# Cross-attention with image-prompt keys on one Trainium2 core: the last query chunk and the last key chunk of an odd batch moved ahead of the next batch's projections

## The chip, the cores and the metric

The kernel runs on one core of one Trainium2 chip. A core has a matrix engine (TensorE, in the profile PE, with its weight loads listed apart as PEld), a vector engine (VectorE, DVE), a scalar engine (ScalarE, ACT), GpSimd (POOL) and a queue engine that issues transfers (SyncE, SP). The metric is the device time of one execution in microseconds. Before the change the median of three runs is 409.02 us (408.52 to 409.29).

## The reference, cut to what matters

Eight batches (B = 8), 112 queries each (S), 375 context rows of 512 channels (T, E): 371 text rows and 4 image-prompt rows. C = 320 channels in H = 20 heads of 16.

```python
q = heads(hidden_states @ W_q);  k_t = heads(text_ehs @ W_k);  v_t = heads(text_ehs @ W_v)
probs_t = softmax(q @ k_t.T * Dh ** -0.5)
text_out = probs_t @ v_t
k_ip = heads(ip_ehs @ W_k_ip);  v_ip = heads(ip_ehs @ W_v_ip)
attn_scores = q @ k_ip.T * Dh ** -0.5
qsem = l2norm(probs_t @ text_ehs)              # per head, 512 channels
sem = qsem @ l2norm(ip_ehs).T
probs_ip = softmax(attn_scores + 0.5 * sem) * spatial_mask
out = (text_out + probs_ip @ v_ip) @ W_out + b_out + hidden_states
```

The norm of `qsem` is never formed from its 512 channels. With G = text_ehs @ text_ehs.T it is the sum of p * (G p), so the kernel multiplies the transposed probabilities by a matrix that holds G, the prompt products and the head's values side by side.

## The kernel before, in words

All data are float32. The work is a run of 40 steps (b, g): batch b, group g of four heads, five groups a batch. One step does the following.

* `scores` (line 789): four matmuls, one for each head of the group, into four PSUM banks. They read `kT`, the batch's transposed keys in three chunks of channels, and `qm`, its masked queries, in the same three chunks. Groups 0 to 3 read chunks 0 and 1. Group 4 alone reads the last chunk.
* `probabilities`: DVE takes the row maximum (802), ACT the exponential (806) and a small copy of the prompt columns (808), and SP writes the result into the buffer `xg` (813). After the copy the PSUM bank is free.
* `transposed` (825): DVE turns `xg` into `xgT`.
* `product` (837): 12 blocks j of four matmuls each, `xgT` by `u`, into four PSUM banks `ps_qd`. `u` is filled by transfers (547) and by POOL copies of the values (`placed`, 755).
* `value_sums` (ACT, 864) and `reduced` (DVE, 890) read the four banks and so free them.

The order of every engine's instructions is written out by hand; nothing is scheduled by a planner. After the first step the loop takes two steps at a time. `pair` issues the products of the two steps, and during the first two blocks of the first one the scores of the step that comes two later. Between pairs `behind` issues all other matrix work: projections of queries, keys and values, the Gram matrix G, and the pieces of `finish`, a generator (called as `f`) that ends a batch step by step. `q`, `k` and `v` are such generators too, one chunk a call. In the branch that the change touches, `k(nb)` is a chunk of the next batch's keys with a copy on ACT (563, 570), `v(nb)` the seven block products of the next batch's values (`two_chunks`, 663) with seven copies on ACT (664) and seven sums on POOL (667), `q(b)` the last chunk of this batch's queries, scaled on DVE (376, 386), and `k(b)` the last chunk of this batch's keys, copied by ACT in four parts (580, 590). `tr(0)` transposes all of the coming step, `tr(1)` half of the one after it.

That branch runs behind group 1 of every odd batch except the last: for b = 1, 3 and 5. The pair that follows starts with step (b, 2), and the scores in it are those of (b, 4), the group that reads the last chunks.

There are eight PSUM banks in three pools: four `qd`, two `sc`, two `mm`. The list `turn` names the pool from which each call of `bank` in `behind` takes its bank, in order. A bank can be written again when its last reader is done.

ACT switches between two tables, for square roots and for exponentials, with explicit loads (`preload_act_table`, lines 1427 and 1432 in this branch).

Of the kernel before, what the change touches and what calls it, by code (L numbers as in the profile page):

```python
# [9 lines left out]
AF = mybir.ActivationFunctionType  # L10
# [10 lines left out]
def kernel(  # L21
# [14 lines left out]
    nc = tc.nc  # L36
# [52 lines left out]
    turn = []  # L89
# [258 lines left out]
    def turned_inputs(bs, i0=0, i1=NC):  # L348

        t0, n = blocks_of(bs)  # L350
        if bs[0] not in inputs_turned:
            inputs_turned[bs[0]] = work.tile(
                [P, NC, 2 * S], F32, tag="xT", name=f"xT_{bs[0]}", bufs=1
            )
        xT = inputs_turned[bs[0]]
        nc.vector.transpose(
            xT[:, i0:i1, : n * RG].rearrange("p i (j r) -> p j i r", r=RG),
            x_in[:, :n, i0 * RG : i1 * RG].rearrange("p j (i c) -> p j i c", c=RG),
        )
# [53 lines left out]
    def load_next(b):  # L413
        if 2 <= b < B:
            loaded[b] = load_ctx(b)
# [127 lines left out]
    def gram_to_groups(b, blocks, eng=nc.sync):  # L543

        for q in blocks:
            for a in range(GROUP):
                eng.dma_start(
                    st[b]["u"][a * RG : (a + 1) * RG, q * GW : (q + 1) * GW],
                    ug[q * RG : (q + 1) * RG, :],
                )  # L550
# [5 lines left out]
    def keys(b):  # L556
        s = st[b]
        if b > 1:
            prompt_keys(b)
        for i in range(FULL):  # L560
            ps = bank(f"ps_k_{b}_{i}")
            for e in range(NE):
                nc.tensor.matmul(  # L563
                    ps[:, :TT],
                    wk_sb[:, e, i * P : (i + 1) * P],
                    s["ctxT"][:, e, :TT],
                    start=(e == 0),
                    stop=(e == NE - 1),
                )
            nc.scalar.copy(s["kT"][:, i, :TT], ps[:, :TT])  # L570
            yield
        last_keys(b, bank(f"ps_k_{b}_{FULL}", spare=0 < b < B - 1))
        yield
# [21 lines left out]
    def values(b):  # L595
        s = st[b]
        s["vext"] = work.tile([P, NT, C], F32, tag="vext", name=f"vext_{b}", bufs=1)
        ctxT, vext = s["ctxT"], s["vext"]
        if b > 1 and b % 2 == 0:
            two_chunks(b)  # L600
            yield
        for c in range(0 if b < 2 else 2, NT):
            ps = bank(f"ps_v_{b}_{c}")
            for e in range(NE):
                nc.tensor.matmul(  # L605
                    ps[:, :C],
                    ctxT[:, e, c * P : (c + 1) * P],
                    wv_sb[:, e, :],
                    start=(e == 0),
                    stop=(e == NE - 1),  # L610
                )
            nc.scalar.copy(vext[:, c, :], ps[:, :C])
            yield
        if b > 1 and b % 2:
            two_chunks(b)
            yield
# [98 lines left out]
    def prompt_values(b):  # L715

        nc.sync.dma_start(
            st[b]["vip"].rearrange("p n h d -> p (n h d)"),
            vipd[b * NIP : (b + 1) * NIP, :].rearrange("n c -> (n c)").partition_broadcast(S),
        )  # L720
# [94 lines left out]
    def transposed(b, g, j0=0, j1=BLK):  # L815

        xg = x_ring[(b * NG + g) % NX]
        if j1 < j0 + 1:
            return
        if ("xT", g) not in st[b]:  # L820
            st[b]["xT", g] = work.tile([P, BLK, P], F32, tag="xgT", name=f"xgT_{b}_{g}")
        xT = st[b]["xT", g]
        n = BLK // (2 if b == B - 1 or (b, g) == (0, 0) or j1 - j0 < BLK else 1)
        for j in range(j0, j1, n):
            nc.vector.transpose(  # L825
                xT[:, j : j + n].rearrange("p j (k q) -> p q j k", q=QN),
                xg[:, :, j * RG : (j + n) * RG].rearrange("p q (j k) -> p q j k", k=RG),
            )
# [317 lines left out]
    def run(key, make, pieces=1):  # L1146

        if key not in gens:
            gens[key] = make()
        for _ in range(pieces):  # L1150
            next(gens[key], None)
# [56 lines left out]
    def f(b, pieces=1):  # L1208
        if b >= 0:
            run(("f", b), lambda: finish(b), pieces)  # L1210

    def k(b, pieces=1):
        run(("k", b), lambda: keys(b), pieces)

    def v(b, pieces=1):
        run(("v", b), lambda: values(b), pieces)

    def gr(b, pieces=1):
        run(("g", b), lambda: gram(b), pieces)
# [116 lines left out]
    def behind(n):  # L1336

        b, g = steps[n]
        nb = b + 1
        two = steps[n + 1 : min(n + 3, len(steps) - NG + 1)]  # L1340

        def tr(i):
            if i < len(two):
                transposed(*two[i], 0, BLK // (1 + i))

        if b % 2 == 0 and g == 0:
            if n == 0:
                turn[:] = ["sc", "sc", "mm"]
                turned_inputs(pairs[1])
            else:  # L1350
                turn[:] = ["qd"] * 4 + ["mm"]
                k(b)
                nc.scalar.preload_act_table(AF.Sqrt)
                f(b - 1)
                if b - 1 < B - 2:
                    prompt_values(b - 1)
            if n:
                token_sums(nb)
                gr(nb)
                tr(0)  # L1360
            if n:
                gr(nb, 2)
                f(b - 1)
            v(nb)
            if n == 0:
                k(nb)
                run(("pp",), prompt_projections)
            if n:
                tr(1)
                f(b - 1, 2)  # L1370
            load_next(b + 2)
        elif b % 2 == 0 and g == 2:
            turn[:] = ["qd"] * (8 if b else 3) + ["mm"]
            gram_to_groups(nb, (2,))
            if b == 0:
                run(("pp",), None)
                prompt_keys(nb)
                tr(0)
                v(nb)
                q(nb)  # L1380
                values_to_dram(nb, nc.scalar, 0, 2)
                v(nb)
                values_to_dram(nb, nc.scalar, 2)
                run(("pp",), None)
            else:
                values_to_dram(nb, nc.gpsimd, 2)
                k(nb)
                tr(0)
                v(nb)
                q(nb)  # L1390
                values_to_dram(nb, nc.gpsimd, 0, 2)
            tr(1)
        elif b % 2 == 0 and nb < B - 1:
            turn[:] = ["qd"] * (4 + (b > 0)) + ["mm", "mm"]
            turned(b + 2)
            token_sums(b + 2)
            q(nb)
            if b > 0:
                f(b - 1)
            else:  # L1400
                run(("t", b), lambda: prompt_logits(b))
            k(nb)
            tr(0)
            if b > 0:
                f(b - 1)
            gr(nb + 1, 3)
            if b > 0:
                f(b - 1)
            if n + 1 not in late:
                tr(1)  # L1410
            load_next(b + 3)
            f(b)
            prompt_values(b)
        elif b % 2 == 0:
            turn[:] = ["qd"] * 4 + ["mm"]
            q(nb, 2)
            f(b - 1)
            k(nb)
            nc.scalar.preload_act_table(AF.Sqrt)
            tr(0)  # L1420
            f(b - 1, 2)
            prompt_values(b)
            f(b, 2)
        elif g == 1:
            turn[:] = ["qd"] * 8 + ["sc", "mm"]
            gram_to_groups(nb, (2,))
            nc.scalar.preload_act_table(AF.Sqrt)
            f(b - 1)
            k(nb)
            tr(0)  # L1430
            v(nb)
            nc.scalar.preload_act_table(AF.Exp)
            q(b)
            k(b)
            f(b - 1)
            tr(1)
            f(b - 1)
            values_to_dram(nb, nc.sync, 0, 2)
            if b == B - 3:
                prompt_values_by_head()  # L1440
        else:
            turn[:] = ["qd"] * 3 + ["sc"]
            load_turned(nc.gpsimd, pairs[(b + 3) // 2])
            v(nb)
            f(b - 1)
            values_to_dram(nb, nc.sync, 2)
            tr(0)
            k(nb)
            f(b - 1, 2)
            tr(1)  # L1450
            gram_to_groups(nb, (3,))
            values_to_groups(nb, 2)
        assert not turn, (b, g, turn)

    for n in range(0, len(steps) - NG, 2):
# [4 lines left out]
        b, g = steps[n]  # L1460
# [16 lines left out]
    b = B - 1  # L1477
# [125 lines left out]
```

## Time and profile before

| | |
|---|---|
| median of three runs | 409.02 us |
| the profiled execution | 407.42 us |
| its span, first to last instruction | 405.7 us |
| PE busy | 398.3 us (98% of the span) |
| DVE busy | 329.1 us (81%) |
| ACT busy | 198.8 us (49%) |
| POOL busy | 182.8 us (45%) |
| granted TensorE clock | 0.999 |
| the branch's stretch, from its first key matmul to the next pair's first product | 95.24 to 103.71, 191.67 to 200.15, 287.46 to 295.93 us |

Times inside the profile are microseconds from the first instruction. A busy PE is one that has a matmul in flight, which is less than one at its peak. A row of a timeline reads: start, duration, engine, line, operation, output and inputs, shape, count, and in brackets the idle time before it with what ended it. In the chain of waits, the work that ended last is followed back from the end; a row is start, duration and what it was.

### The profile page before, as it was taken

What the parts mean: (1) busy time and instruction counts of PE and PEld (TensorE: products, weight loads), DVE (VectorE), ACT (ScalarE), POOL (GpSimd) and SP (SyncE); (2) the same over time, 40 slices, a digit from 0 to 9 for tenths busy, and PEclk for the clock granted to TensorE, in tenths of its full rate; (3) what the DMA queues carried; (4) which work ended last, traced back from release to release, by engine and by line L of the source; (5) the groups of instructions that cost most, each with busy time, mean ns of one, the idle gap of its engine ahead of it and who ended that gap; (6) DMA issues with size and microseconds to landing.
All of it is one profiled execution on the core that took longest, in us unless ns stands there. A gap on an engine that the chain in (4) does not pass through costs nothing.

```text
span 405.7 us, 14386 instructions
## 1 busy us (share of the span) xinstructions
PE 398.3 (98%) x5673; PEld 322.0 (79%) x5673; DVE 329.1 (81%) x703; ACT 198.8 (49%) x707; POOL 182.8 (45%) x391
## 2 busy tenths in 40 slices
PE   8999999999999999999999999999999999999996
PEld 7868688888777887978786878878877878887894
DVE  4457689866998897987899898897789898888984
ACT  3245332336542843525653564334654385446764
POOL 8735012063281558141554338523337155804681
PEclk9999999999999999999999999999999999999999
DMA  8969756969665966577647766667856444776311
GB/s 244 228 179 251 138 154 169 206 137 215 159 173 153 215 148 178 135 180 165 179 122 171 182 170 167 161 164 163 190 141 169 121 124 110 190 176 175 110 53 28
DMA packets 58390, 65.85 MB, mean 162 GB/s; under 512 B 20165, under 2 KB 51641, under 8 KB 58324
## 3 DMA queue, kind: packets, MB, share of 16 engines
q1 hardware_dynamic: 54814, 58.23, 57.7%
q0 software_dynamic: 2336, 5.42, 5.5%
q10 hardware_dynamic: 1174, 1.29, 1.0%
q8 instruction: 45, 0.74, 0.8%
q14 instruction: 21, 0.17, 0.2%
HBM read 20.22 MB, written 5.22 MB: 63 GB/s over the span
## 4 chain that ended last, share of the span: by engine, by line
PE 92%; DMA 4%; POOL 1%; ACT 1%; DVE 0%; issue 0%; POOLq 0%
PE ps_qd L837 44%; PE ps_k L563 10%; PE ps_s L789 7%; PE ps_g L533 7%; PE ps_v L605 7%; PE ps_vs L663 6%; PE ps_o L994 3%; PE ps_k L580 3%; PE ps_q L394 3%; DMA xg<-p 2%; DMA vr<-vd 1%; PE ps_g L495 1%; ACT kT L590 1%; DMA ct<-in_ctx_dram 1%; PE ps_c L464 1%; PE ps_a L985 1%
## 5 line engine op out<-in xcount | busy, mean ns | idle before, releaser
L837 PE MATMUL ps_qd<-u,xgT 32*112 32x232 f32 (+11 forms) x3840 | 217.8, 352 | 0.6 <-POOL u L755 0.5
L837 PEld LDWEIGHTS ps_qd<-u,xgT 32*112 32x112 f32 x3840 | 179.9, 172 | 31.7 <-issue 4.2
L825 DVE STREAM_TRANSPOSE xgT<-xg 128x768 f32<-128x768 f32 (+1 forms) x63 | 123.1, 1972 | 5.4 <-DMA xg<-p 4.7
L806 ACT ACTIVATE p<-ps_s,nmx 112x371 f32<-112x371 f32 x160 | 85.5, 585 | 63.0 <-DVE nmx L802 62.0
L802 DVE TENSOR_REDUCE nmx<-ps_s 112x1 f32<-112x371 f32 x160 | 76.8, 533 | 28.3 <-PE ps_s L789 26.7
L755 POOL COPY u<-vr 128x64 f32<-128x64 f32 x120 | 27.1, 238 | 159.8 <-PE ps_qd L837 90.0
L890 DVE CUSTOM_DVE_ANT_0 p<-ps_qd,p 112x371 f32<-112x371 f32 x152 | 73.5, 541 | 11.9 <-ACT pvs L864 7.4
L789 PE MATMUL ps_s<-kT,qm 32*112 32x375 f32 (+1 forms) x320 | 61.5, 487 | 1.6 <-ACT kT L590 1.6
L864 ACT COPY pvs<-ps_qd 112x21 f32<-112x21 f32 x152 | 21.8, 200 | 55.8 <-DVE ss L890 50.1
L563 PE MATMUL ps_k<-ctxT,wk_sb 128*128 128x371 f32 x128 | 43.4, 482 | 0.0
L789 PEld LDWEIGHTS ps_s<-kT,qm 32*112 32x112 f32 x320 | 27.4, 171 | 9.2 <-ACT kT L590 3.5
L563 PEld LDWEIGHTS ps_k<-ctxT,wk_sb 128*128 128x128 f32 x128 | 23.1, 190 | 12.2
L533 PE MATMUL ps_g<-ctxT 128*32 128x119 f32 (+11 forms) x672 | 32.7, 338 | 0.0
L533 PEld LDWEIGHTS ps_g<-ctxT 128*32 128x32 f32 x672 | 27.7, 109 | 6.1 <-POOL ctxT L440 0.9
L605 PE MATMUL ps_v<-wv_sb,ctxT 128*128 128x320 f32 x96 | 28.3, 441 | 0.0
L452 DVE STREAM_TRANSPOSE ctxT<-ct 128x512 f32<-128x512 f32 x21 | 22.5, 1084 | 4.1 <-DMA ct<-in_ctx_dram 4.1
L808 ACT COPY ipl<-ps_s 112x4 f32<-112x4 f32 x140 | 24.3, 173 | 0.0
L605 PEld LDWEIGHTS ps_v<-wv_sb,ctxT 128*128 128x128 f32 x96 | 17.5, 190 | 6.6
L570 ACT COPY kT<-ps_k 128x371 f32<-128x371 f32 x16 | 7.5, 466 | 23.1 <-PE ps_k L563 23.1
L973 POOL TENSOR_TENSOR vip<-vip,w 112x1280 f32<-112x1280 f32 (+1 forms) x8 | 17.5, 2182 | 0.2 <-DVE w L967 0.2
L517 POOL TENSOR_TENSOR ug<-ug,half 128x128 f32<-128x128 f32 (+1 forms) x24 | 10.6, 447 | 14.3 <-ACT ug L516 11.7
L512 ACT ACTIVATE ug<-ps_g 128x279 f32<-128x279 f32 (+5 forms) x24 | 8.0, 333 | 18.3 <-PE ps_g L533 13.4
(179 smaller groups left out, 439.4 us busy)
## 6 DMA issues: line engine op xcount, KB each, us to landing
xg<-p SPq DMA_DIRECT2D x159, 162.3 KB
u<-ug SPq DMA_DIRECT2D x120, 99.0 KB
ct<-in_ctx_dram SPq DMA_DIRECT2D x28, 176.0 KB
vip<-vipd SPq DMA_DIRECT2D x7, 560.0 KB
vr<-vd SPq DMA_DIRECT2D x20, 120.0 KB
out_dram<-ob SPq DMA_DIRECT2D x7, 140.0 KB
vr<-vd SPq DMA_DIRECT2D x12, 80.0 KB
x_in<-in_x_dram POOLq DMA_DIRECT2D x12, 70.0 KB, 3.7
```

The source lines that it names most:

```text
L533: nc.tensor.matmul(ps[p * RG : (p + 1) * RG, s0 : T - t0], ctxT[:, e, t0 + q * RG : t0 + (q + 1) * RG], ctxT[:, e, t0 + s0 : T], start=(e ...
L563: nc.tensor.matmul(ps[:, :TT], wk_sb[:, e, i * P : (i + 1) * P], s["ctxT"][:, e, :TT], start=(e == 0), stop=(e == NE - 1),)
L605: nc.tensor.matmul(ps[:, :C], ctxT[:, e, c * P : (c + 1) * P], wv_sb[:, e, :], start=(e == 0), stop=(e == NE - 1),)
L663: nc.tensor.matmul(ps[:, :CH], a[:, k], t[:, k], start=(k == 0), stop=(k == 1))
L755: nc.gpsimd.tensor_copy(region(b, c)[:, :, UV - c * P :], s["vr"][:, c * QN : (c + 1) * QN, g, :])
L789: nc.tensor.matmul(ps[:S, :w], qm[a * RG : (a + 1) * RG, i, r, j * S : (j + 1) * S], s["kT"][a * RG : (a + 1) * RG, i, :w], start=True, st ...
L802: nc.vector.tensor_reduce(nmx, ps[:S, :TT], AX.X, ALU.max, negate=True)
L806: nc.scalar.activation(p, ps[:S, :TT], AF.Exp, bias=nmx)
L808: nc.scalar.copy(s["ipl"][:, groups[g][a], :], ps[:S, TT:T])
L825: nc.vector.transpose(xT[:, j : j + n].rearrange("p j (k q) -> p q j k", q=QN), xg[:, :, j * RG : (j + n) * RG].rearrange("p q (j k) -> p ...
L837: nc.tensor.matmul(banks[a][:S, j * RG : UW], xT[a * RG : (a + 1) * RG, j, :S], region(b, c)[a * RG : (a + 1) * RG, p, q * RG :], start=(j ...
L890: nc.vector.tensor_tensor_reduce(out=p, in0=ps[:S, :TT], in1=p, scale=1.0, scalar=0.0, op0=ALU.mult, op1=ALU.add, accum_out=s["ss"][:, h : ...
```

## The change

Inside the branch for group 1 of an odd batch, the calls are put in another order. `q(b)` and `k(b)` come first, ahead of `k(nb)` and `v(nb)`. One call of `f(b - 1)` (the one that takes the square root and starts `zr`, `attn` and `xb`) now stands behind them and not at the start; the next call stands ahead of `v(nb)` and not behind `k(b)`. The load of the exponential's table comes right behind the square root. `turn` gives the ten banks so that the first seven are `qd` and the last three block products take `sc`, `mm` and `mm`; before, the first eight were `qd`, the queries took `sc` and the keys `mm`. No instruction is added or removed.

```diff
         elif g == 1:
-            turn[:] = ["qd"] * 8 + ["sc", "mm"]
+            turn[:] = ["qd"] * 7 + ["sc", "mm", "mm"]
             gram_to_groups(nb, (2,))
             nc.scalar.preload_act_table(AF.Sqrt)
-            f(b - 1)
-            k(nb)
-            tr(0)
-            v(nb)
-            nc.scalar.preload_act_table(AF.Exp)
             q(b)
             k(b)
             f(b - 1)
+            nc.scalar.preload_act_table(AF.Exp)
+            k(nb)
+            tr(0)
+            f(b - 1)
+            v(nb)
             tr(1)
             f(b - 1)
             values_to_dram(nb, nc.sync, 0, 2)
```

On PE, for b = 1, between the last product of step (1, 1) and the first scores of (1, 4). Before:

```order
L837 MATMUL ps_qd_1_1_1257<-u_274,xgT_1_1218 112x40
L563 MATMUL ps_k_0_1384<-ctxT_972,wk_sb 128x371 x4
L663 MATMUL ps_vs_1397<-wv_sb,ctxT_972 128x160 x2
...
L663 MATMUL ps_vs_1427<-wvt,ctxT_972 128x160 x2
L376 MATMUL ps_q_2_1433<-xT_589,wq_sb 64x112 x6
L580 MATMUL ps_k_2_1444<-ctxT_271,wk_sb 64x186
...
L837 MATMUL ps_qd_2_0_1472<-u_274,xgT_2_1390 112x392
...
L789 MATMUL ps_s_2_1480<-kT_272,qm_844 112x375
```

The same place now:

```order
L837 MATMUL ps_qd_1_1_1257<-u_274,xgT_1_1218 112x40
L376 MATMUL ps_q_2_1378<-xT_589,wq_sb 64x112 x6
L580 MATMUL ps_k_2_1389<-ctxT_271,wk_sb 64x186
...
L563 MATMUL ps_k_0_1409<-ctxT_972,wk_sb 128x371 x4
L663 MATMUL ps_vs_1429<-wv_sb,ctxT_972 128x160 x2
...
L663 MATMUL ps_vs_1459<-wvt,ctxT_972 128x160 x2
L837 MATMUL ps_qd_2_0_1472<-u_274,xgT_2_1415 112x392
...
L789 MATMUL ps_s_2_1480<-kT_272,qm_844 112x375
```

The six query matmuls and the eight matmuls of the last key chunk (one row of the eight is shown) moved from the end of the stretch to its start; the scores that read them stay where they were.

On ACT, from the load of the square root's table to the exponential of `finish`. Before:

```order
L1427 ACT_TABLE_LOAD
L939 ACTIVATE rn_1173<-rn_1173 112x20
L570 COPY kT_973<-ps_k_0_1384 128x371
L664 COPY v_2_1393<-ps_vs_1397 128x160
...
L664 COPY vext_1392<-ps_vs_1427 128x160
L1432 ACT_TABLE_LOAD
L590 COPY kT_272<-ps_k_2_1444 64x186 x2
L590 COPY kT_272<-ps_k_2_1444 64x185 x2
L959 ACTIVATE ex_1466<-fu_1458 112x80
```

Now:

```order
L1427 ACT_TABLE_LOAD
L590 COPY kT_272<-ps_k_2_1389 64x186 x2
L590 COPY kT_272<-ps_k_2_1389 64x185 x2
L939 ACTIVATE rn_1173<-rn_1173 112x20
L1431 ACT_TABLE_LOAD
L570 COPY kT_973<-ps_k_0_1409 128x371
L664 COPY v_2_1425<-ps_vs_1429 128x160
...
L664 COPY vext_1424<-ps_vs_1459 128x160
L959 ACTIVATE ex_1466<-fu_1418 112x80
```

The four copies into this batch's `kT` and the second table load moved ahead of the copy of the next batch's keys and of all seven copies of block products.

On DVE, in the same stretch, behind the four reductions of step (1, 1), as a difference:

```order
+L386 TENSOR_SCALAR qm_844<-ps_q_2_1378,emask 64x112 x4
 L942 RECIPROCAL zr_1175<-pvs_172 112x20
-L825 STREAM_TRANSPOSE xgT_2_1390<-xg_142 128x4x384
-L386 TENSOR_SCALAR qm_844<-ps_q_2_1433,emask 64x112 x4
+L825 STREAM_TRANSPOSE xgT_2_1415<-xg_142 128x4x384
 L949 RECIPROCAL rn_1173<-rn_1173 112x20
```

The four scalings into `qm` moved from behind the transposition of the coming step to a place ahead of it and of `zr`. POOL and SP keep their order.

## The prediction

> **What bounds the kernel now.** I read the page's busy times and chain first, then who waited for whom on PE, then the chain in order of time around the three places of the branch (b = 1, 3, 5; sites 1 to 3), then their timelines.
>
> ```profile
> PE 398.3 (98%) x5673; PEld 322.0 (79%) x5673; DVE 329.1 (81%) x703; ACT 198.8 (49%) x707; POOL 182.8 (45%) x391
> PE 92%; DMA 4%; POOL 1%; ACT 1%; DVE 0%; issue 0%; POOLq 0%
> PE ps_s L789 <- ACT kT L590: 1.6, 3, 0.5
> PEld ps_s L789 <- ACT kT L590: 3.5, 3, 1.2
> ```
>
> PE has almost no idle time and is 92% of the chain, so only what removes a stall of PE can help. The largest repeated one is three waits of scores for the copies of the last key chunk, one a site. PE counts 1.6 us idle, its weight loads 3.5 us; the true loss lies between, since matmuls are in flight for part of it. It can be read from the length of a whole pair. The chain in order of time:
>
> ```profile
> 102.53 1.28 PE ps_k L580 x16
> 105.16 0.57 PE ps_s L789 x2
> 115.90 2.35 PE ps_v L605 x8
> 141.65 1.15 PE ps_qd L837 x10
> 152.35 2.69 PE ps_k L563 x8
> 198.96 1.28 PE ps_k L580 x15
> 211.69 2.35 PE ps_v L605 x8
> 294.75 1.28 PE ps_k L580 x16
> 307.47 2.35 PE ps_v L605 x8
> ```
>
> A pair without this wait runs from 141.65 to 152.35, 10.70 us. The pairs behind the sites run from the end of their last key matmuls: 103.81 to 115.90 (12.09), 200.24 to 211.69 (11.45), 296.03 to 307.47 (11.44). All issue the same products and scores. So the excess is 1.39, 0.75 and 0.74 us, 2.88 in all. That is the most that the change can win here.
>
> **The change part by part.** Site 2 shows every part; its timeline:
>
> ```profile
> 191.67 2.76 PE L563 MATMUL ps_k<-ctxT,wk_sb 128*128 128x371 f32 x8
> 192.61 0.44 ACT L864 COPY pvs<-ps_qd 112x21 f32<-112x21 f32 x4
> 193.07 1.28 ACT L1427 ACT_TABLE_LOAD   x1
> 194.27 0.71 PE L663 MATMUL ps_vs<-wv_sb,ctxT 128*128 128x160 f32 x4
> 194.36 0.22 ACT L939 ACTIVATE rn<-rn 112x20 f32<-112x20 f32 x1
> 194.49 0.45 ACT L570 COPY kT<-ps_k 128x371 f32<-128x371 f32 x1
> 194.71 0.28 DVE L942 RECIPROCAL zr<-pvs 112x20 f32<-112x20 f32 x1
> 194.90 2.95 DVE L825 STREAM_TRANSPOSE xgT<-xg 128x1536 f32<-128x1536 f32 x1
> 196.44 0.71 PE L663 MATMUL ps_vs<-wv_sb,ctxT 128*128 128x160 f32 x4
> 198.17 0.80 PE L376 MATMUL ps_q<-xT,wq_sb 128*64 128x112 f32 x12
> 198.28 0.29 ACT L664 COPY vext<-ps_vs 128x160 f32<-128x160 f32 x1 [0.25 <-PE ps_vs L663]
> 198.79 1.42 PE L580 MATMUL ps_k<-ctxT,wk_sb 128*64 128x186 f32 x16
> 199.01 1.39 DVE L386 TENSOR_SCALAR qm<-ps_q,emask 64x112 f32<-64x112 f32 x4 [1.16 <-PE ps_q L376]
> 200.15 0.93 PE L837 MATMUL ps_qd<-u,xgT 32*112 32x392 f32 x8
> 200.27 1.27 ACT L590 COPY kT<-ps_k 64x186 f32<-64x186 f32 x4 [0.40 <-PE ps_k L580]
> 200.44 0.28 DVE L949 RECIPROCAL rn<-rn 112x20 f32<-112x20 f32 x1
> 201.59 0.57 PE L789 MATMUL ps_s<-kT,qm 32*112 32x375 f32 x2 [0.52 <-ACT kT L590]
> 201.75 1.57 DVE L825 STREAM_TRANSPOSE xgT<-xg 128x768 f32<-128x768 f32 x1
> ```
>
> *PE's stretch.* From start to start: next keys 2.60, seven block products 3.90, queries 0.62, last keys 1.36, together 8.48. In the new order queries start at 191.67, last keys at 192.29, next keys at 193.65, block products at 196.25, one each 0.54 ((196.44 - 194.27) / 4), and the first product again at 200.15. Changing the shape of the weights costs a little at each border; three borders are replaced by three others. I take 0; the largest idle time of the weight loads at such a border is quoted below (0.27 us), so the bound is 0.27 either way a site, 0.8 in all.
>
> *The wait itself.* ACT's copies of the last keys come behind the first table load: 194.35 to 195.62. The scales into `qm` follow DVE's last reduction, 194.71 to 196.10. The scores that need both come behind the product of 200.15. The wait of 0.75 is gone.
>
> *The new wait on ACT.* The copy of the next keys now stands behind four key copies (1.27), the square root (0.22) and the second load (1.28): 195.62, 195.84, 197.12, and with 0.45 it ends at 197.57. It frees a bank that a later block product takes: with four `qd` banks the fourth block product, due at 196.25 + 3 x 0.54 = 197.87. Margin 0.3 us. Queued behind this copy are the seven copies of block products. The first is due at about 197.0 and is 0.6 late, then they catch up at 0.29 each against PE's 0.54. Before, the seventh started on PE at 194.27 + 6 x 0.54 = 197.53 and its copy at 198.28; 1.98 later that copy ends at 200.55. Its `mm` bank is wanted by the scores of block 1, behind the 0.93 us of block 0, past 201. Cost 0; bounds 0 and what the slow rival below costs.
>
> *DVE.* `zr` and the transposition of the coming step slide back by 1.39: 196.3 to 199.3, and the product that needs it is at 200.15. At site 1 DVE idles before that transposition (first row of the next fence), which hides the scaling. What stood behind the scaling comes earlier: the five small operations of `finish` start at 199.3 and not 200.44, so the half transposition starts at 200.6 and not 201.75.
>
> *POOL and SP.* POOL's `attn` comes 1.39 us later, behind `zr`, and the sums of the block products at most the 1.98 us by which these move. SP's writes of the values wait for the sums, and behind them in its queue stand the rows of (b, 4). At site 3:
>
> ```profile
> 290.68 2.95 DVE L825 STREAM_TRANSPOSE xgT<-xg 128x1536 f32<-128x1536 f32 x1
> 296.29 2.22 SPq L699 DMA_DIRECT2D vd<-vext  x4
> 300.30 2.69 SPq L813 DMA_DIRECT2D xg<-p  x3
> ```
>
> At worst the writes start at 298.3 and end at 300.5, and the rows follow about a microsecond later than now. PE wants them in the pair that begins after 307.47. Cost 0.
>
> *Site 1's second excess.*
>
> ```profile
> 100.50 3.06 DVE L825 STREAM_TRANSPOSE xgT<-xg 128x1536 f32<-128x1536 f32 x1 [1.95 <-DMA xg<-p]
> 103.71 0.29 PEld L837 LDWEIGHTS ps_qd<-u,xgT 32*112 32x112 f32 x8 [0.27 <-POOL vext L667]
> 106.07 1.56 DVE L825 STREAM_TRANSPOSE xgT<-xg 128x768 f32<-128x768 f32 x1
> 107.67 1.89 DVE L802 TENSOR_REDUCE nmx<-ps_s 112x1 f32<-112x371 f32 x4
> 110.23 0.21 ACT L808 COPY ipl<-ps_s 112x4 f32<-112x4 f32 x1
> 110.49 2.33 PEld L837 LDWEIGHTS ps_qd<-u,xgT 32*112 32x112 f32 x41 [0.26 <-ACT ipl L808]
> ```
>
> Of site 1's 1.39 us, 0.75 is the wait for the keys. The other 0.64 is the second step's products, which wait for the banks of the scores, and these wait for row maxima that stand behind the half transposition of 106.07 on DVE. When PE comes 0.75 earlier it meets this wait again unless DVE is earlier too. By the order DVE would start it at 104.87 (103.56 + 1.31, the length of the five operations, 200.44 to 201.75), 1.20 earlier; but the rows of `xg` at this site arrive late (DVE already waited 1.95 us for the first set), and when the second set lands no row tells. Bounds: not earlier at all, gain 0; 1.20 earlier, gain 1.2. I take the middle, 0.6. At sites 2 and 3 DVE did not idle for rows (194.90 and 290.68 stand without a wait), so they get their whole 0.75 and 0.74.
>
> *Sum:* 0.6 + 0.75 + 0.74 = 2.1 us. The profiled execution is 407.42 us (span 405.7), 1.6 below the median of 409.02; it would become 405.3, the median 406.9.
>
> **The rivals.** *Taken back at the score banks* (no change). The wait of site 1 appears at all sites if DVE's half transposition does not come earlier; then the 0.75 only moves it. For it: DVE is close behind PE in these pairs, and site 1 shows the wait. Against it: the 1.16 us for which DVE waited for the queries disappears. The half transposition starts 1.60 us behind the pair's first product at site 2 (201.75 - 200.15) and 2.36 at site 1, which is 0.64 short; so site 2 has 0.12 to spare, and only that is won: 0.12 each at sites 2 and 3, 0 at site 1, 408.8.
>
> *The key copy behind two table loads* (slower). If ACT loses time at each load, the fourth block product waits. It decides from a copy that ends later than 197.8; past 198.8 (2.88 / 3 more) it eats the whole gain. Each load costing its own length again (1.28, the nearest row) puts the copy at 200.13 and the wait at 2.3 a site: 6.9 - 2.9 = 4.0 more, 413. One load of the two doing so gives 1.0 a site and ends within 0.5 us of before. Against it: the square root starts at 194.36, 0.01 behind the load of 193.07, and that load 0.02 behind the copy before it.
>
> [...]
>
> *That the change does not do what it says* needs PE to start the scores before the moved work; the order of the rows on PE, shown with the change, excludes it.
>
> **How the numbers follow.** Forecast 0.76 (site 1's gain between 0 and 1.2: 1.5 to 2.7 us, with the borders' 0.8 either way 405.5 to 408.3), taken back at the banks 0.13, one late load 0.04, two 0.07. A measurement of this kernel can tell about 0.2%, 0.8 us, from no change. Faster 0.76, same 0.17, slower 0.07. The range goes from 405.8 to 408.8, which holds the case of the banks too.
>
> **What would show it.** Right: no wait of scores for kT L590; the pairs behind sites 2 and 3 at 10.70; the stretch at 8.48 and the key copy ending 5.9 us into it; site 1's pair between 10.9 and 12.1, with the wait for the copy L808 still there. Wrong: idle time of PE ahead of a block product (the load), or a wait for L808 at sites 2 and 3 (the banks).

## The result, and the profile after

The changed kernel takes 406.50 us (median of 22 runs, 404.78 to 408.93) against 408.24 us before (22 runs, 406.55 to 412.97): ratio 0.996, 95% interval 0.9945 to 0.9975, about 1.6 us less (1.0 to 2.2). The forecast was 2.1 us less, 406.9 us from the 409.02 of three runs. The profiled execution took 405.13 us, its span 403.4 (before 407.42 and 405.7), so 2.3 us less.

The page of the changed kernel, busy times and chain of waits, and then the longest row of its table of who waited for whom on PE:

```profile
PE 398.0 (99%) x5673; PEld 321.9 (80%) x5673; DVE 331.3 (82%) x703; ACT 198.5 (49%) x707; POOL 182.7 (45%) x391
PE 97%; POOL 1%; DMA 1%; issue 0%; ACT 0%; SPq 0%; POOLq 0%
PE ps_w L481 <- POOL ident masks.py:199: 1.4, 1, 1.4
```

PE's busy time is as before (398.3). No wait of the scores for L590 is left, and none of their weight loads. Site 2 in the changed kernel's timeline:

```profile
190.35 0.80 PE L376 MATMUL ps_q<-xT,wq_sb 128*64 128x112 f32 x12
190.98 1.42 PE L580 MATMUL ps_k<-ctxT,wk_sb 128*64 128x186 f32 x16
192.33 2.76 PE L563 MATMUL ps_k<-ctxT,wk_sb 128*128 128x371 f32 x8
193.04 1.27 ACT L590 COPY kT<-ps_k 64x186 f32<-64x186 f32 x4
194.57 1.28 ACT L1431 ACT_TABLE_LOAD   x1
194.93 0.71 PE L663 MATMUL ps_vs<-wv_sb,ctxT 128*128 128x160 f32 x4
195.87 0.47 ACT L570 COPY kT<-ps_k 128x371 f32<-128x371 f32 x1
198.83 1.22 PE L837 MATMUL ps_qd<-u,xgT 32*112 32x392 f32 x10
199.54 1.59 DVE L825 STREAM_TRANSPOSE xgT<-xg 128x768 f32<-128x768 f32 x1
```

The stretch is 8.48 us (190.35 to 198.83). The copy of the next keys ends at 196.34, 5.99 us into it (forecast 5.9). The four copies of the last keys end at 194.31, 4.5 us before the pair begins; before, they ended 1.4 us behind its start. The half transposition starts 0.71 us behind the pair's first product, before 1.60.

The chain in order of time gives the pairs: behind site 1, behind site 2 and the pair after it, then the same two at site 3.

```profile
99.98 3.80 PE ps_vs L663 x28
114.48 2.35 PE ps_v L605 x8
195.09 3.80 PE ps_vs L663 x28
209.59 2.35 PE ps_v L605 x8
216.36 1.15 PE ps_qd L837 x10
227.06 1.40 PE ps_k L580 x15
290.10 3.80 PE ps_vs L663 x28
304.60 2.35 PE ps_v L605 x8
311.37 1.15 PE ps_qd L837 x10
322.60 1.40 PE ps_k L580 x14
```

From the end of the block products, the pairs behind the three sites take 10.70, 10.70 and 10.70 us (114.48 - 103.78, 209.59 - 198.89, 304.60 - 293.90). From the first product on PE, before against after: 12.12 to 10.70, 11.47 to 10.70 and 11.47 to 10.70, which is 1.42 + 0.77 + 0.77 = 2.96 us won. But the pair that follows site 3's own takes 11.23 (311.37 to 322.60), where the same pair at site 2 takes 10.70 (216.36 to 227.06): 0.53 us are given back. Another 0.10 goes to the pair at 121.18, behind site 1's own (10.80). With the start of the program (nothing net) that is the 2.3 us of the spans. The timeline around the pair at 311:

```profile
313.01 1.58 DVE L825 STREAM_TRANSPOSE xgT<-xg 128x768 f32<-128x768 f32 x1 [1.05 <-DMA xg<-p]
317.19 2.33 PEld L837 LDWEIGHTS ps_qd<-u,xgT 32*112 32x112 f32 x41 [0.26 <-ACT ipl L808]
```

DVE stands 1.05 us until its rows have landed; the row maxima behind it come late, so do the exponentials and ACT's copy L808, and the products of the second step wait for the banks of the scores. It is the mechanism that the prediction found at site 1 of the kernel before, at a new place. What is late is SP, which issues the rows; its queue at site 3 in the changed kernel, and then the last three lines of the same piece before:

```profile
295.52 2.71 SPq L699 DMA_DIRECT2D vd<-vext  x4
298.28 0.77 SPq L724 DMA_DIRECT2D vipx<-vipd  x1
299.16 3.58 SPq L813 DMA_DIRECT2D xg<-p  x4
302.85 3.15 SPq L708 DMA_DIRECT2D vr<-vd  x4
306.10 3.53 SPq L813 DMA_DIRECT2D xg<-p  x4
```

```profile
300.30 3.58 SPq L813 DMA_DIRECT2D xg<-p  x4
303.99 1.97 SPq L708 DMA_DIRECT2D vr<-vd  x4
307.22 3.53 SPq L813 DMA_DIRECT2D xg<-p  x4
```

Before, the four writes of values (296.29, in the prediction) and the 0.77 us of `vipx` ended at 299.3, and SP paused for 0.98 us ahead of the rows of 300.30 and for 1.26 ahead of those of 307.22. After, it works from 295.52 to 309.6 with hardly a gap. The rows for the pair in question (the last line of each) moved up by 1.1 us, PE by 2.9: their lead over that pair's first product shrank from 6.95 us (314.17 - 307.22) to 5.20 (311.30 - 306.10).

### The profile page after: what moved, and what is told of

Its sections match the earlier page's. It is cut to its first block, busy times and chain, and to the rows that moved or that the text cites. A ratio compares the mean times of both kernels' runs of the same rounds, so it can differ in the third digit from the quotient of the medians.

```text
span 403.4 us, 14380 instructions
## 1 busy us (share of the span) xinstructions
PE 398.0 (99%) x5673; PEld 321.9 (80%) x5673; DVE 331.3 (82%) x703; ACT 198.5 (49%) x707; POOL 182.7 (45%) x391
## 3 DMA queue, kind: packets, MB, share of 16 engines
q10 hardware_dynamic: 1174, 1.29, 1.0%
## 4 chain that ended last, share of the span: by engine, by line
PE 97%; POOL 1%; DMA 1%; issue 0%; ACT 0%; SPq 0%; POOLq 0%
PE ps_qd L837 46%; PE ps_k L563 10%; PE ps_g L533 8%; PE ps_v L605 7%; PE ps_s L789 6%; PE ps_vs L663 6%; PE ps_q L394 3%; PE ps_o L994 3%; PE ps_k L580 3%; PE ps_g L495 1%; DMA ct<-in_ctx_dram 1%; PE ps_a L985 1%; PE ps_q L376 1%; PE ps_c L464 0%; POOL attn L980 0%; PE ps_o L1086 0%
## 5 line engine op out<-in xcount | busy, mean ns | idle before, releaser
L837 PE MATMUL ps_qd<-u,xgT 32*112 32x40 f32 (+11 forms) x3840 | 216.9, 352 | 0.2
L808 ACT COPY ipl<-ps_s 112x4 f32<-112x4 f32 x140 | 24.3, 174 | 0.0
```

What stands on the lines that cost most here:

```text
L808: nc.scalar.copy(s["ipl"][:, groups[g][a], :], ps[:S, TT:T])
L837: nc.tensor.matmul(banks[a][:S, j * RG : UW], xT[a * RG : (a + 1) * RG, j, :S], region(b, c)[a * RG : (a + 1) * RG, p, q * RG :], start=(j ...
```

## The experiments

**The kernel before, once more.** No edit.

> The kernel before, profiled a second time. My theory: the three waits of scores for the copies of the last keys (pairs behind sites 2 and 3 at 11.45 to 11.47 us against 10.70) are fixed by the order and come back within 0.02 us; site 1's second excess of 0.64 us depends on when its rows of xg land and may be anything from 0 to 0.7. Rival: the excesses vary all alike from one execution to the next, and then the difference of two profiles tells nothing.

One run of 408.58 us. The pairs behind the sites took 11.72, 11.47 and 11.47 us. At sites 2 and 3 the excess is fixed to some hundredths from one execution to the next; site 1's second excess was 0.25 and not 0.64. There the half transposition started 1.95 us behind the pair's first product (105.83 - 103.88) instead of 2.36. The full transposition before it, which waits for rows in both profiles, started 3.60 us ahead of the pair (100.28) instead of 3.21 (100.50). So this term belongs to the execution: the landing of rows sets it.

The two pairs behind site 1's own took 10.89 and 11.59 us here, where the first profile had 10.70 twice. In both DVE waited for rows; in the second pair:

```profile
142.32 1.56 DVE L825 STREAM_TRANSPOSE xgT<-xg 128x768 f32<-128x768 f32 x1 [1.82 <-DMA xg<-p]
```

and the products of its second step waited for L808. So in the order of before, too, rows can come late behind site 1, and then they cost PE 0.19 + 0.89 = 1.08 us.

**Only the queries and keys first; load and second finish late as before.** The edit is shown against the kernel before.

```
-            turn[:] = ["qd"] * 8 + ["sc", "mm"]
+            turn[:] = ["qd"] * 7 + ["sc", "mm", "mm"]
             ...
+            q(b)
+            k(b)
             f(b - 1)
             k(nb)
             tr(0)
             v(nb)
             nc.scalar.preload_act_table(AF.Exp)
-            q(b)
-            k(b)
             f(b - 1)
```

> Queries and last keys first as in the change, but the exponential's table load and the second call of finish behind the block products, as in the kernel before. My theory: only the waits for the last keys were worth anything, so the scores wait for nothing, the pairs behind the sites are at 10.70 us and the time is that of the change, 0.996 of before. Rival, that the earlier load and the earlier call of finish are part of the gain: pairs over 11 us or a time nearer to 1.000.

406.61 us, ratio 0.9965 (0.9942 to 0.9988), like the whole change. Pairs behind the sites: 11.27, 10.70, 10.70; the pair that follows site 3's took 11.33. At site 1 the stretch took 8.68 and the pair behind its own 11.13. The early table load and the earlier second part of `finish` have no share in the gain that can be told.

**Only the keys first; the queries stay last.**

```
             nc.scalar.preload_act_table(AF.Sqrt)
+            k(b)
             f(b - 1)
             ...
             q(b)
-            k(b)
             f(b - 1)
```

> Only the last keys are moved to the front; the last queries stay behind the block products. My theory: the wait for the keys' copies goes, but DVE still scales the queries late, so its half transposition still starts 1.6 us behind the pair's first product and the second step's products wait about 0.6 us for the banks of the scores (ACT L808) at sites 2 and 3: pairs at 11.3 us, gain 0.1 to 0.15 us a site, ratio 0.999 to 1.000. Rival, that the keys' copies alone set the price: pairs at 10.70 us and 0.996.

411.95 us, ratio 1.0094 (1.0066 to 1.0123): 0.9% slower than before. Pairs behind the sites 12.64, 12.63 and 12.63, stretches 8.62. Timeline of site 2, whose pair starts at 201.29:

```profile
200.56 0.80 PE L376 MATMUL ps_q<-xT,wq_sb 128*64 128x112 f32 x12
201.41 1.39 DVE L386 TENSOR_SCALAR qm<-ps_q,emask 64x112 f32<-64x112 f32 x4 [2.54 <-PE ps_q L376]
204.15 1.57 DVE L825 STREAM_TRANSPOSE xgT<-xg 128x768 f32<-128x768 f32 x1
208.58 2.33 PEld L837 LDWEIGHTS ps_qd<-u,xgT 32*112 32x112 f32 x41 [0.26 <-ACT ipl L808]
```

In its table of waits the scores wait for the scaled queries and no longer for L590:

```profile
PEld ps_s L789 <- DVE qm L386: 1.7, 3, 0.6
```

Less gain than from the whole change was expected, but still a gain of 0.1 to 0.15 us a site, and not a loss. With the last keys taken from between them, the queries end right before the pair, and DVE, which idles 2.54 us for them, scales them inside it. The queries start 0.73 us ahead of the pair's first product and not 1.98 as before. The half transposition starts 2.86 us behind the pair's first product (before 1.60), and everything behind it is late: PE waits for banks of scores (L808) and for copies of `u` (0.53 us). This is the rival "taken back at the score banks", made real: with the wait for L590 gone, DVE's lead decides next. The size is that of this order, which also pushed DVE 1.26 us back; what the removed wait is worth with DVE where it was before, no run shows. Queries first is the half that gives DVE its lead.

**Only the queries first; the last keys stay last.**

```
             nc.scalar.preload_act_table(AF.Sqrt)
+            q(b)
             f(b - 1)
             ...
-            q(b)
             k(b)
             f(b - 1)
```

> Only the last queries are moved to the front; the last keys stay behind the block products. My theory: the scores wait for the keys' copies as before, pairs behind sites 2 and 3 at 11.45 to 11.47 us, ratio 0.999 to 1.000 (site 1's second excess may go, up to 0.6 us). Rival, that the place of the queries' scaling on DVE is what counts: pairs at 10.70 us and 0.996.

408.66 us, ratio 1.0022 (1.0004 to 1.0039). Pairs 11.66, 11.66 and 11.66, stretches 8.79. The waits on PE:

```profile
PE ps_s L789 <- ACT kT L590: 2.1, 3, 0.7
```

The wait for the keys stays, as expected, but it is longer (2.1 us for 1.6 before), and the pairs are 0.2 us longer than the 11.45 to 11.47 forecast for sites 2 and 3. Site 1 takes no longer than the others: its second excess is gone. The two halves alone are 0.2% and 0.9% slower than before; together they are 0.4% faster. Keys first leaves the queries' way through DVE as the bound, queries first the keys' way through ACT. Why the stretch grew by 0.31 us was not followed.

**The changed kernel, once more.** No edit.

> The changed kernel once more, with a profile, beside the three kernels below. Theory: the three pairs behind the sites take 10.70 us each whatever the execution, since what they had waited for (the copies of the last keys) ends 4 us ahead; what varies between executions is transfers. And of the 2.9 us that PE gains, about half a microsecond is given back in the pair right behind the one of site 3, because SP issues the rows for it only 1.1 us earlier while PE arrives 2.9 us earlier: that pair takes 11.2 to 11.4 us again and DVE's half transposition in it waits about 1 us for its rows. Rival: the 11.23 us of the first profile was an accident of that one execution's transfers; then that pair takes 10.70 now. Time: 406.5, ratio to before 0.996.

406.13 us, ratio 0.9947 (0.9915 to 0.998). Pairs behind the sites 11.00, 10.70, 10.70. The pair that follows site 3's took 11.86, DVE waited 1.68 us in it:

```profile
296.50 3.68 SPq L699 DMA_DIRECT2D vd<-vext  x4
307.56 3.53 SPq L813 DMA_DIRECT2D xg<-p  x4
314.61 1.57 DVE L825 STREAM_TRANSPOSE xgT<-xg 128x768 f32<-128x768 f32 x1 [1.68 <-DMA xg<-p]
```

So it is no accident of one execution, and longer than the 11.2 to 11.4 expected. SP needed 3.68 us for the four writes of values that took it 2.22 before, and the lead of the rows was 4.72 us (312.28 - 307.56).

**Two more table loads ahead of the key copy.** They cost ACT time and nothing needs them. This edit and the next two are shown against the changed kernel.

```
             nc.scalar.preload_act_table(AF.Exp)
+            nc.scalar.preload_act_table(AF.Sqrt)
+            nc.scalar.preload_act_table(AF.Exp)
             k(nb)
```

> The changed kernel with two more table loads (square root, exponential) ahead of the copy of the next pair's keys at each site; nothing else is changed and nothing needs them. They measure the margin and the price of the slow rival of the prediction (the key copy behind table loads holds a bank of the block products). Theory: the loads take 1.28 us each and nothing follows them, so the copy ends at 5.99 + 2.56 = 8.55 us into PE's stretch; the fourth block product, which takes its bank, is due at 6.2 and waits 2.3 us. Each stretch goes from 8.47 to about 10.8, the time rises by 3 x 2.3 = 7 us to about 413.5, ratio to before 1.013. [...] Rival 2 (the copy isn't what the block products wait for, and the margin is large): stretches stay at 8.5, time 406.5.

416.06 us, ratio 1.0145 (1.0069 to 1.0222), four runs. Stretches 11.96, 12.12 and 12.29 instead of the expected 10.8, the pairs behind them 11.36, 11.19 and 11.03. Site 2's timeline, then two of its windows (length, then busy time of PE, PEld, DVE, ACT and POOL, granted TensorE clock, DMA share, GB/s):

```profile
199.25 1.28 ACT L1432 ACT_TABLE_LOAD   x1
200.54 1.28 ACT L1433 ACT_TABLE_LOAD   x1
201.83 0.47 ACT L570 COPY kT<-ps_k 128x371 f32<-128x371 f32 x1
202.35 0.81 PE L663 MATMUL ps_vs<-wvt,xs 128*128 128x160 f32 x4 [2.25 <-ACT kT L570]
203.59 1.27 PE L663 MATMUL ps_vs<-wv_sb,xs 128*128 128x160 f32 x4
```

```profile
200.10:202.35 2.25, 0.00 (x1) 0.00 (x0) 2.11 (x6) 2.23 (x4) 0.15 (x2) 1.00 0.67 158
...
203.60:205.86 2.26, 2.26 (x10) 1.93 (x9) 0.36 (x1) 0.58 (x2) 2.01 (x5) 0.50 0.00 0
```

Two findings. The first is the one expected: the fourth block product waits for the bank that the key copy holds, 2.25 us (expected 2.3), so the margin of the changed kernel is 2.56 - 2.25 = 0.3 us, as the prediction had it. The loads follow each other after 1.29 us, and the copy starts 0.01 us behind the last. The second was not expected: 1.14 us after PE works again (0.97 to 1.32 over the three sites) its granted clock falls to 0.50, and a block product of four matmuls takes 1.27 us and not 0.71. This costs another 1.4 us of the stretch and half a microsecond of the pair; at each of the three sites the two together are 1.9 us, only differently divided.

**One transfer out of SP's way.** The load of the prompt's values by head moves from site 3 to the end of the branch that follows.

```
             values_to_dram(nb, nc.sync, 0, 2)
-            if b == B - 3:
-                prompt_values_by_head()
         else:
             ...
+            if b == B - 3:
+                prompt_values_by_head()
```

> The changed kernel with the one transfer of prompt values by head (0.77 us of SP's time at site 3) issued some 10 us later, at the end of the branch that follows, so that SP comes 0.8 us earlier to the rows that the pair behind site 3's pair waits for. Theory (SP's queue is late there): DVE's half transposition in that pair waits about 0.3 us and not 1.05, the pair takes 10.7 us and not 11.2 to 11.4, and the time falls by up to 0.5 to about 406.0. Rival (the transfers themselves take longer there, whatever SP does): the pair keeps its 11.2 to 11.4, the time stays at 406.5.

405.31 us, ratio 0.9926 (0.9889 to 0.9963), nine runs. The pair that follows site 3's took 10.70, DVE waited 0.45 us in it:

```profile
305.85 3.53 SPq L813 DMA_DIRECT2D xg<-p  x4
312.65 1.57 DVE L825 STREAM_TRANSPOSE xgT<-xg 128x768 f32<-128x768 f32 x1 [0.45 <-DMA xg<-p]
```

As the theory of SP's queue had it. The lead was 5.70 us (311.55 - 305.85), and a wait of 0.45 of DVE cost PE nothing. This is one profile, and between executions of the changed kernel itself the lead varies by half a microsecond (table below), so alone it would not decide; the next edit moves the lead by more.

**The writes of values by POOL.** SP does not wait for POOL's sums any more.

```
-            values_to_dram(nb, nc.sync, 0, 2)
+            values_to_dram(nb, nc.gpsimd, 0, 2)
```

> The changed kernel with the first four writes of values at the sites issued by POOL, which computes them, instead of SP, so that SP does not wait for the sums of the block products. Theory (SP waits for POOL's sums, 10.2 us behind the start of site 3's pair count, and all its rows come behind that wait): the rows of the pair behind site 3's pair come about 2 us earlier, that pair takes 10.7, time about 406.0 (0.5 less) if POOL bears the issues. Rival 1 (the transfers and not the queue): that pair keeps 11.2 to 11.4. Rival 2: four issues hold POOL for about 2 us right behind its sums, its copies of u in the pair behind the site come up to 1 us late, PE waits for them, and the pairs behind the sites go from 10.70 to as much as 11.7, so that the time rises by up to 3 us.

405.74 us, ratio 0.9918 (0.9887 to 0.9949). All pairs behind the sites and the ones that follow them took 10.70. POOL's and SP's issues and DVE's half transposition:

```profile
295.60 2.08 POOL L699 DMA_DIRECT2D vd<-vext  x4
303.93 3.55 SPq L813 DMA_DIRECT2D xg<-p  x4
311.56 1.56 DVE L825 STREAM_TRANSPOSE xgT<-xg 128x768 f32<-128x768 f32 x1
```

The rows are issued 2.2 us earlier than in the changed kernel's first profile, the lead is 7.05 us, DVE does not wait, and POOL bears the four issues without making PE wait.

**The changed kernel, a third time, and the writes by POOL, a second time, on one chip.**

> The changed kernel once more, as the measure on this chip for the two kernels that follow. Theory: pairs behind the sites 10.70 us behind sites 2 and 3 again, the pair right behind site 3's pair between 11.2 and 11.9 us (11.23, 11.33 and 11.86 in three profiles so far), time 406.1 to 406.6, ratio to before 0.995 to 0.9965.

406.72 us, ratio 0.9978 (0.9961 to 0.9994). Pairs behind the sites 10.70 each; the pair that follows site 3's took 11.64, and the one that follows site 1's 11.56, where PE waited for a copy of `u` whose transfer came late:

```profile
126.54 0.42 POOL L755 COPY u<-vr 128x64 f32<-128x64 f32 x2 [7.42 <-DMA vr<-vd]
```

> The changed kernel with the first four writes of values issued by POOL, once more, beside a second timing of the changed kernel on the same chip. Theory (SP's queue at the sites took back a part of the gain): every pair behind a site and the one behind it take 10.70 us, the time is 0.5 to 1.2 us below that of the changed kernel, about 405.3 to 405.9. Rival (the first timing was scatter): no difference from the changed kernel beyond 0.2%.

406.48 us, ratio 0.996 (0.9942 to 0.9979). Again every pair at and behind the sites took 10.70. In time, the difference from the changed kernel here is 0.2 us of the medians; the first time it was 0.4. Taking both chips together, 24 runs each, the means are 405.91 and 406.70 us: 0.8 less, with an interval of 0.2 to 1.4 by resampling these runs. So it is probably faster than the changed kernel, but by the medians alone the expected 0.5 to 1.2 us is not shown; what the traces show is that the wait is gone. Whether it is better than the run with the prompt values later (405.31 us beside its own 405.74) is not shown.

**The kernel before with the writes by POOL.** The same one-line edit, the order of before.

> The kernel before with only this edit: the first four writes of values at the sites are issued by POOL instead of SP; the order of PE's work is that of before. Theory (SP's lateness only matters once PE has won its 2.9 us): the pairs behind sites 2 and 3 keep 11.47 us, the pair right behind site 3's pair keeps its 10.70, so next to nothing is won: 407.6 to 408.3, ratio 0.998 to 1.000 (up to 0.5 us from site 1's second excess, which varied between 0.25 and 0.64). Rival (the edit is worth about 1 us by itself, whatever the order): ratio 0.997 or below.

408.25 us, ratio 1.0002 (0.998 to 1.0025). Pairs 12.10, 11.47 and 11.47; the pair that follows site 3's 10.70 as before. By itself the edit has no gain that can be told. At site 3 the reason is in the traces: there SP's lateness becomes a cost only once PE is earlier. Behind site 1 this profile lost nothing, like the first profile of before and unlike the second.

**One more load of the same table.** Against the changed kernel.

```
             nc.scalar.preload_act_table(AF.Exp)
+            nc.scalar.preload_act_table(AF.Exp)
             k(nb)
```

> The changed kernel with one more table load (exponential again) ahead of the copy of the next pair's keys at each site; nothing needs it. With two more loads PE stood still for 2.25 us a site and then, which the theory had not foreseen, its granted clock fell to 0.50 for about 3.3 us, so that a site lost 3.65 us. With one load the copy ends 1.28 us later and PE should stand still for 1.28 - 0.22 = 1.0 us at the third or fourth block product. [...] Theory B (any standstill of a microsecond halves the clock for 3.3 us): the stretches go to about 11, the time to 413 or 414.

The trace has the two loads of each site, L1427 and L1431 (1.28 us each), and none for the added line. So this told nothing of a standstill of one microsecond; that stays open. It is one more profile and timing of the changed kernel: 406.83 us, ratio 0.9972 (0.995 to 0.9995), pairs 11.41, 10.70, 10.70, and 11.78 for the pair that follows site 3's. At site 1 DVE waited 0.91 us for rows.

The pair that follows site 3's, over the profiles (starts from the timelines, us):

| kernel | rows issued | pair's first product | lead | DVE waits | pair |
|---|---|---|---|---|---|
| before | 307.22 | 314.17 | 6.95 | 0 | 10.70 |
| before, again | 308.08 | 315.02 | 6.94 | 0 | 10.70 |
| before, writes by POOL | 307.11 | 314.06 | 6.95 | 0 | 10.70 |
| changed | 306.10 | 311.30 | 5.20 | 1.05 | 11.23 |
| changed, load and finish late | 307.36 | 312.38 | 5.02 | 1.15 | 11.33 |
| changed, again | 307.56 | 312.28 | 4.72 | 1.68 | 11.86 |
| changed, third | 307.35 | 312.07 | 4.72 | 1.45 | 11.64 |
| changed (load that fell out) | 307.55 | 312.14 | 4.59 | 1.60 | 11.78 |
| prompt values later | 305.85 | 311.55 | 5.70 | 0.45 | 10.70 |
| writes by POOL | 303.93 | 310.98 | 7.05 | 0 | 10.70 |
| writes by POOL, again | 304.73 | 311.80 | 7.07 | 0 | 10.70 |

With a lead of 5.7 us or more there is no excess; at 5.2 and below it is there in every profile.

## Why the prediction was right, and where it was not

The time (406.50 for 406.9 forecast, within 405.8 to 408.8) and the sign came out as forecast, and the gain has the stated reason: the scores' wait for the last keys is gone. That the number lies so near is in part luck, as the sum below shows. By its steps:

- *PE's stretch, cost 0.* 8.47 to 8.48 at all three sites, before and after. The new borders cost what the old ones did: where the shape of the weights changes, PEld idled 0.17 us ahead of the queries and 0.27 ahead of the first product before, and 0.27 us ahead of the next keys and 0.17 ahead of the first product after, at every site.
- *The wait itself, 0.75 and 0.74 at sites 2 and 3.* Gone, 0.77 each in every profile.
- *The new wait on ACT, margin 0.3.* The copy ended 5.99 us into the stretch for 5.9, and the extra loads measured the margin as 0.3. ACT lost nothing beyond the 1.28 us of each load: at site 2 the copy starts 0.02 us behind the second load's end (195.87 - 195.85).
- *DVE's half transposition 1.15 to 1.2 earlier.* At site 2 it starts at 199.54 and not 201.75, which against the pair's first product is 0.89 earlier (0.71 behind it for 1.60). That is 0.26 less than forecast, but enough that no bank of scores holds PE. The keys-only run shows what depends on it: with 2.86 instead, the pair takes 12.63.
- *Site 1's second excess, 0.6 as the middle of 0 to 1.2.* In four profiles of the changed kernel its pair took 10.70, 10.70, 11.00 and 11.41, in two of before 12.12 and 11.72: on average 11.92 - 10.95 = 0.97 won. The average lies inside the bounds, with the middle too low. The sign that the prediction named, a pair of 10.9 to 12.1 with the wait for L808 still there, held in two of the four. In the other two the pair took 10.70; in the first of them the rows came in time (DVE's full transposition started without a wait) and the whole 1.42 was won, more than the upper bound of 1.2, which had kept the late rows of before.
- *POOL and SP, cost 0.* This is the term that was mis-sized. It asked when the rows of (b, 4) are wanted and found time enough, but not what stands behind those rows in SP's queue: the reads of the values and the rows of the step after. At site 3 these are late by 1.05 to 1.68 us for DVE and cost 0.53 to 1.16 us of PE, 0.93 on average over four profiles. The pairs after site 1's lose too, 0.10, 0.64, 0.86 and 0 us, 0.40 on average; but in the two profiles of before they lost 0 and 1.08, so this loss is not shown to come from the change.

The two errors partly cancel: the forecast had 0.6 + 0.75 + 0.74 = 2.1; the profiles give 0.97 + 0.77 + 0.77 = 2.5, less 0.93 at site 3, so 1.6. The four timings of it, by their ratios, say 1.6, 2.2, 0.9 and (the load that fell out) 1.1 us. The base helped as well: the 409.02 of three runs stood 0.8 above the 408.24 of 22, and from 408.24 the same sum would have given 406.1.

Of the rivals, "taken back at the score banks" had the right mechanism in the wrong place: not in the pairs behind the sites, where DVE's lead suffices, but one pair on, where the rows set DVE's start. The price of the slow rival (413 at 2.3 us a site) was too low: with a standstill of that length the kernel took 416, because the granted clock fell to 0.50 as well, which cost 1.9 us more a site. The condition of that rival, loads that cost their length twice, did not arise: the loads followed each other after 1.29 us.

## What to carry to other kernels

When PE's stall is removed, follow each queue that feeds the next steps (here SP's issues) for two steps on, not one: the gain arrived there as a shorter lead (5.20 us for 6.95), and SP, with hardly a gap from 295.52 to 309.6, moved its rows up by 1.1 us where PE moved by 2.9. Two ways to the same matmul that end at nearly the same time (keys on ACT, queries through DVE) had to be moved together; each alone lost time here. An edit that is worth nothing before a change can be worth something after it, so queues should be looked at again once the bound has moved.

## What the runs showed of the hardware

In one run a standstill of PE cost more than its length. With two more loads PE stood 2.25 us at each site; the granted clock stayed at 1.00 for another 0.97 to 1.32 us of work and then was 0.50, and at each site that cost 1.9 us more. The windows of that run in which it falls, at sites 1, 2 and 3, and the one in which it comes back at site 2:

```profile
104.30:105.00 0.70, 0.70 (x5) 0.70 (x5) 0.66 (x1) 0.33 (x2) 0.52 (x1) 0.65 0.70 166
203.40:203.60 0.20, 0.20 (x4) 0.20 (x3) 0.20 (x1) 0.15 (x1) 0.00 (x0) 0.72 0.40 120
302.20:302.50 0.30, 0.30 (x4) 0.30 (x4) 0.30 (x1) 0.09 (x1) 0.25 (x1) 0.96 0.21 53
...
206.80:207.00 0.20, 0.20 (x8) 0.16 (x4) 0.00 (x0) 0.00 (x0) 0.05 (x1) 0.74 0.00 0
```

At site 2 it was halved from about 203.49 to 206.90, 3.4 us, beginning 3.39 us after PE had stopped (200.10). By the share of each window that was halved, it fell at 104.51 and 302.48 at the other sites, 3.57 and 3.22 us after the stops at 100.94 and 299.26, and there, too, for 3.4 us. So the falls lie 98.98 and 98.99 us apart and the stops 99.16: the fall does not follow the stop at a fixed distance. What sets its moment and its length is not shown, and one run alone has it. The fall came three times out of three, each time behind 2.25 us of standstill between dense work (at site 2 PE was busy for all of the 4.40 us before it and the 1.25 us behind it). The waits of 0.5 us in the kernel before left the clock at 1.00 (site 2, 199 to 206 us). What a standstill between 0.5 and 2.25 us does to the clock there was not measured.

At site 3 SP's issue of one and the same set of four writes took 2.22 us in both profiles of before and 2.71 to 3.77 in four of the changed kernel. In the first of these a single issue took 1.25 us; in the first profile of before none took over 0.57. At site 1 the set took 2.21 to 2.33 us in these four. What holds the issue at site 3 was not found.
